# Down projection by halves, two additions left to PSUM, and list masks made as signs on ScalarE

## The chip, the cores and the metric

The kernel runs on one core of a Trainium2 chip. The metric is the device time of one execution in microseconds (us). Throughout, PE is TensorE (its weight loads are shown apart as PEld), DVE is VectorE, ACT is ScalarE, POOL is GpSimd and SP is SyncE, the queue that issues the plain loads and stores. A line number such as L680 is a line of the kernel before.

## The reference

Four sequences of 2048 tokens with 256 features pass through a routed feed-forward layer at half weight, an attention layer and the same feed-forward layer again. The change lies in the two feed-forward layers, which are alike. Each sends every token to two of eight experts; an expert takes the 1280 tokens of its list.

```python
x = x + 0.5 * _L0_ffn_ref(_layernorm(x), router_w, wg, wu, wd)
x = x + _L0_attn_ref(_layernorm(x), Wq, bq, Wk, bk, Wv, bv, Wo, bo)
x = x + 0.5 * _L0_ffn_ref(_layernorm(x), router_w, wg, wu, wd)
# in _L0_ffn_ref, for each expert e and the rows of its list:
g = jnp.einsum('ecd,edf->ecf', disp, wg)                  # 256 -> 1024
u = jnp.einsum('ecd,edf->ecf', disp, wu)                  # 256 -> 1024
eo = jnp.einsum('ecf,efd->ecd', jax.nn.silu(g) * u, wd)   # 1024 -> 256
# each row of eo is multiplied by the token's weight and added to the token's row of the output
```

All of these products are in float32.

## The kernel before

**Chunks and units.** The function `experts` (called once for each feed-forward layer) works through 16 chunks: eight experts, two chunks each, a chunk being 5 tiles of 128 tokens (640 columns, two halves of 320). An expert's chunks are called even (first) and odd (second) below. A chunk has an up stage (`steps_of`) and a down stage (the loop over `order` at the end of `experts`). The up stage has four units `p`. In each unit a 2x2 block product of gate and of up is made from seven half-size products instead of eight: seven pairs of matmuls of 320 columns (`both` is one pair, the gate and the up), with sums of weight blocks (`sums_of_w`, kept in `ws`) and sums of input blocks (`sums_of_x`, kept in `xs`). The results of the pairs are put together by seven additions on DVE, out of PSUM into the tile `ct` (four quadrants of gate and up) by way of `u2`; ACT applies silu to the gate quadrants, and `finish` multiplies gate by up into `h`, on POOL for the first three units and on DVE for the last.

**Down stage.** For each of the 5 token tiles, 8 matmuls of 256 columns are summed in PSUM (h as the stationary side, the expert's `wd` as the moving side). ACT then scales the tile by the tokens' weights into `eo`, and POOL adds it to the tokens' rows in DRAM by an indirect DMA.

**Tokens in.** POOL fetches the rows of a chunk by five indirect DMAs (`gather`, tiles `r`), ACT blanks unused rows (`blank`), PE turns them (`turn`, transposes through the PSUM bank `tr`) and ACT copies them to `xsT`.

**Lists.** `RowList` makes the next expert's list of rows during the even chunk. `high` makes `hi` and `hv` in three DVE instructions; `low(g)`, eight of them, makes a 0/1 mask of 8 x 128 columns from each token's slot number by comparing with a counter on DVE (L395); `products(g)` multiplies the masks in by eight small matmuls; `sum` and `end` bring the sums out, turn them and give the indices `ixs`, for which the gathers of the next expert wait. `behind` places these steps between the token tiles of the down stage. The first list of a layer is made ahead of the chunks by another form of the same functions (`waited_for`).

**Buffers.** In PSUM a pair of banks `mm` is held three times over, `one` and `tr` once each. In SBUF `ct` is held twice: unit `p + 2` writes where unit `p` wrote, and so has to wait until `finish` has read unit `p`. There are 14 buffers `r` and five for the masks `lo`.

**Order.** The chunks run under a manual schedule, in which PE, DVE, ACT and SP keep the order of the source. POOL is left out of it:

```python
with tc.manual_schedule(engines=ENGINES - {mybir.EngineType.Pool}):
```

so the framework's scheduler orders POOL's multiplications and DMAs among themselves. [...]

Of the kernel before, what the change touches and what calls it, by code (L numbers as in the profile page):

```python
# [26 lines left out]
def macaron_kernel(  # L27
# [84 lines left out]

    row_in = const.tile([P, 1], F32, name="row_in")
# [26 lines left out]
    slot_hi = const.tile([P, E, T], I16, name="slot_hi")  # L140

# [130 lines left out]
    def route(w, pool, ppool, beside=iter(())):  # L272
# [73 lines left out]
        nc.vector.tensor_scalar(slot_lo.rearrange("p e t -> p (e t)"), slot, P - 1, None, ALU.bitwise_and)  # L346

    class RowList:
# [4 lines left out]

        def __init__(self, e, pool, ppool, waited_for=False):
            self.e, self.pool, self.ppool, self.waited_for = e, pool, ppool, waited_for
            self.lo = {}
# [26 lines left out]
        def begin(self):  # L383
            self.ps = self.ppool.tile([P, BANK], F32, tag="one", name="ix", bufs=1)[:, :P]

        def low(self, g):
            lo = self.pool.tile([P, TG * P], F16, tag="lo", name="lo", bufs=5)
            at = slot_lo[:, self.e, g * TG : (g + 1) * TG]
            if self.waited_for:
                lo = lo.rearrange("p (s t) -> p s t", t=TG)  # L390
                nc.vector.tensor_tensor(lo, counts, spread(at.unsqueeze(1), [P, P, TG]), ALU.is_equal)
                self.lo[g] = lo.rearrange("p s t -> p t s")
            else:
                shape, lo = [P, TG, P], lo.rearrange("p (t s) -> p t s", s=P)
                nc.vector.tensor_tensor(  # L395
                    lo, spread(count.unsqueeze(1), shape), spread(at.unsqueeze(2), shape), ALU.is_equal
                )
                self.lo[g] = lo
# [10 lines left out]
        def sum(self):  # L409
            self.sums = self.pool.tile([P, P], F32, tag="sums", name="sums", bufs=2)  # L410
            nc.scalar.copy(self.sums, self.ps)

        def end(self):
            self.ps = self.ppool.tile([P, BANK], F32, tag="tr", name="ixT", bufs=1)[:, :P]
            nc.tensor.transpose(self.ps, self.sums, ident)
            ixf = self.pool.tile([P, HI], F32, tag="ixf", name="ixf", bufs=2)
            nc.vector.tensor_reduce(ixf, self.ps.rearrange("p (g i) -> p i g", i=HI), AX.X, ALU.add)
            ix = self.pool.tile([P, HI], I32, tag="ixs", name="ixs", bufs=3)
            nc.vector.tensor_copy(ix, ixf)
            return ix  # L420
# [17 lines left out]
    def experts(name, src, dst, wait_for, weights, wpool, pool, ppool):  # L438
# [4 lines left out]
        PER = ST // CH  # L443
        assert PER == 2 and ST % CH == 0
        chunks = [(e, i) for e in range(E) for i in range(0, ST, CH)]
        lists, got, xTs, turned, ws, xs = {}, {}, {}, {}, {}, {}
        sent = {-1: list(wait_for)}

        def gather(k):
# [4 lines left out]
            for i in range(i0, i0 + CH):  # L454
                r = pool.tile([P, W], F32, tag="r", name="r", bufs=14)
# [32 lines left out]

        def sums_of_w(e, m):
# [10 lines left out]
            tt(o[:, m, 3, :], a12, o[:, m, 1, :], ALU.subtract)  # L500

# [22 lines left out]
        def steps_of(k):  # L524
# [3 lines left out]
            def product(p, m, ps, j, c, b):  # L528
# [5 lines left out]
                nc.tensor.matmul(ps, a, b, start=True, stop=True)  # L534
# [7 lines left out]
            p1 = {}  # L542

            def first_product(p, m):
                if p == NF:
                    return
                one = ppool.tile([P, BANK], F32, tag="one", name="one", bufs=1)
                product(p, m, one[:, :BH], 0, 0, xT[:, 0, :BH])
                if m == 0:
                    p1[p] = pool.tile([P, 2, BH], F32, tag="p1", name="p1", bufs=2)  # L550
                nc.scalar.copy(p1[p][:, m, :], one[:, :BH])  # L551

            first_product(0, 0)
            for p in range(NF):
# [4 lines left out]
                h = pool.tile([P, 2, CH * P], F32, tag="h", name="h", bufs=NF)  # L559
                hq = h.rearrange("p j (t s) -> p (j t) s", t=2)  # L560
# [4 lines left out]
                def finish(engine, qs):  # L565
                    engine.tensor_tensor(hq[:, qs, :], ct[:, qs, 0, :], ct[:, qs, 1, :], ALU.mult)  # L566

                p2 = both(p, 0, 1, xT[:, 1, :BH])
                if p == 0:
                    first_product(0, 1)  # L570
                    if k == 0:
                        rest_of_first()
                    x4 = xs.pop(k)
                tt(ct[:, 0], p1[p], p2, ALU.add)
                if last:
                    silu(slice(0, 1))
                tt(u2, p1.pop(p), both(p, 1, None, x4[:, 1, :]), ALU.add)
                tt(ct[:, 3], u2, both(p, 2, None, x4[:, 2, :]), ALU.add)
                first_product(p + 1, 0)
                tt(ct[:, 2], ct[:, 3], both(p, 1, 1, x4[:, 3, :]), ALU.add)  # L580
                if last:
                    silu(slice(2, 3))
                p5 = both(p, 0, None, x4[:, 0, :])
                tt(ct[:, 1], u2, p5, ALU.add)
                tt(ct[:, 3], ct[:, 3], p5, ALU.add)
                first_product(p + 1, 1)
                if last:
                    silu(slice(3, 4))
                    finish(nc.vector, slice(0, 4, 2))
                tt(ct[:, 1], ct[:, 1], both(p, 3, None, xT[:, 1, BH:]), ALU.add)  # L590
                if last:
                    silu(slice(1, 2))
                    finish(nc.vector, slice(1, 4, 2))
                else:
                    silu(slice(0, 4))
                    finish(nc.gpsimd, slice(0, 4))
                hs.append(h)
                yield hs

        NL = T // TG  # L600

        def beside(k, p):

            if p == 1:
# [3 lines left out]
            if p > 1:  # L608
                turn(k + 1, p - 2)

        def behind(k, i):

            e, step = chunks[k][0], k % PER
            more = following[0] if e + 1 < E else None
            if step == 0 and more:

                if i == 0:
                    more = following[0] = RowList(e + 1, pool, ppool)
                    more.high()
                    for g in range(3):  # L620
                        more.low(g)
                    more.begin()
                elif i == 1:
                    more.products(0)
                    for g in (3, 4, 5):
                        more.low(g)
                elif i == 2:
                    for g in (1, 2, 3):
                        more.products(g)
                    for g in (6, 7):  # L630
                        more.low(g)
                elif i == 3:
                    for g in (4, 5):
                        more.products(g)
                elif i == 3.5:
                    for g in (6, 7):
                        more.products(g)
                    more.sum()
                elif i == 4:
                    lists[e + 1] = more.end()  # L640
                    gather(k + 2)
            elif step == 1:
                if i in (1, 2):
                    sums_of_w(e + 1, i - 1)
                elif i == 3:
                    gather(k + 2)
            if i in (0, 1):
                turn(k + 1, 2 + i)
            elif i == 2:
                sums_of_x(k + 1)  # L650

        following = [RowList(0, pool, ppool, waited_for=True)]
        first = following[0]
        with tc.manual_schedule(engines=ENGINES - {mybir.EngineType.Pool}):
# [14 lines left out]
            for k, (e, i0) in enumerate(chunks):  # L669
                for p, hs in enumerate(steps_of(k)):  # L670
                    beside(k, p)

                order = [(i, p, j) for i in range(CH) for p in range(NF) for j in range(2)]
                order = sorted(order[: 4 * NF], key=lambda o: (o[1] == NF - 1, o[0])) + order[4 * NF :]
                po = {}
                for i, p, j in order:
                    if i not in po:

                        po[i] = banks()[:, 0, :D]
                    nc.tensor.matmul(  # L680
                        po[i], hs[p][:, j, i * P : (i + 1) * P], weights[e][2][:, j * NF + p, :],
                        start=(p == 0 and j == 0), stop=(p == NF - 1 and j == 1),
                    )
                    if i == CH - 1 and (p, j) == (NF // 2, 0):
                        behind(k, i - 0.5)
                    if p < NF - 1 or j == 0:
                        continue
                    eo = pool.tile([P, D], F32, tag="eo", name="eo", bufs=6)
                    nc.scalar.mul(eo, po[i], got[k][i][:, D + e : D + e + 1])  # L689
                    ins = nc.gpsimd.indirect_dma_start(  # L690
                        out=dst[:, :],
                        out_offset=bass.IndirectOffsetOnAxis(ap=lists[e][:, i0 + i : i0 + i + 1], axis=0),
                        in_=eo, in_offset=None, compute_op=ALU.add,
                    )
                    tc.declare_no_dep(ins.ins, group=f"{name}{e}", reason="an expert's rows are distinct")
                    tc.add_to_no_dep_group(f"{name}{e}", ins.ins)
# [475 lines left out]
```

## Time and profile before

| | us |
|---|---|
| median of three runs (2038.27 to 2040.81) | 2039.37 |
| the profiled execution's own time | 2038.74 |
| its span, first to last instruction | 2036.9 |

| engine | busy us | share of the span |
|---|---|---|
| PE | 1875.8 | 92% |
| PEld | 1440.3 | 71% |
| DVE | 1417.6 | 70% |
| ACT | 657.1 | 32% |
| POOL | 883.1 | 43% |

The span holds a first stage (loading and routing, to about 120 us), the first feed-forward layer (to about 920), attention (to about 1140), routing for the second layer (to about 1235) and the second feed-forward layer. Busy times are of the whole span; in the feed-forward layers the shares differ, and the views by stage show them. Matmuls of float32 appear as two records each, and a group's mean duration of one record is longer than the distance from one record to the next, because they overlap on PE.

### The profile page before, as it was taken

The numbers are of one execution on the slowest core, as the hardware profiler recorded it, in microseconds if no ns is written. First come the engines' busy times: TensorE is split into PE (matmuls) and PEld (weight loads), VectorE is DVE, ScalarE is ACT, GpSimd is POOL, SyncE is SP. The second block draws the span as 40 slices with busy tenths as digits, with TensorE's granted clock in tenths as the row PEclk, the third lists the DMA queues.
The fourth block names the chain that finished last, engine by engine and source line by source line (L and its number), as shares of the span: only waits on it lengthen the run. The fifth ranks groups of instructions, "written<-read, shape, count | busy, mean of one in ns | idle before, by whom it ended". The sixth has DMA issues, their size and how long they took to land.

```text
span 2036.9 us, 24719 instructions
## 1 busy us (share of the span) xinstructions
PE 1875.8 (92%) x9176; PEld 1440.3 (71%) x9176; DVE 1417.6 (70%) x2531; ACT 657.1 (32%) x1325; POOL 883.1 (43%) x737
## 2 busy tenths in 40 slices
PE   6379999999999999998999528999999999999998
PEld 4247777777777777777887415777777777777776
DVE  8867676767676767546798886767676676767654
ACT  5322323232223223225565403232222222232221
POOL 5335353535353535335555303535353535353533
PEclk8589999999999999999999858999999999999999
DMA  9902222223131322115002631313232313131211
GB/s 349 302 28 38 78 40 77 57 59 78 38 80 37 79 40 41 17 16 171 32 32 86 206 111 28 79 37 79 39 82 37 82 37 82 35 85 34 43 14 14
DMA packets 99928, 147.63 MB, mean 72 GB/s; under 512 B 7512, under 2 KB 86368, under 8 KB 99680
## 3 DMA queue, kind: packets, MB, share of 16 engines
q1 hardware_dynamic: 69072, 102.77, 15.0%
q0 software_dynamic: 30720, 43.27, 12.9%
q8 instruction: 73, 1.20, 0.3%
q14 instruction: 47, 0.39, 0.1%
q10 hardware_dynamic: 16, 0.01, 0.0%
HBM read 98.84 MB, written 55.57 MB: 76 GB/s over the span
## 4 chain that ended last, share of the span: by engine, by line
PE 83%; DVE 5%; issue 4%; ACT 1%; POOL 1%; DMA 1%; POOLq 0%; DVEq 0%; ACTq 0%; SPq 0%
PE mm L534 41%; PE mm L680 27%; PE one L534 7%; PE tr L481 2%; PE qp L804 1%; PE pc L859 1%; PE ix L404 1%; PE py L917 1%; DVE st L929 1%; DVE xw L927 1%; DVE q L812 1%; DVE m L817 0%; DVE z L826 0%; DVE st L788 0%; PE trq L847 0%
## 5 line engine op out<-in xcount | busy, mean ns | idle before, releaser
L680 PE MATMUL mm<-wdt,h 128*128 128x256 f32 x2560 | 579.0, 381 | 0.0
L680 PEld LDWEIGHTS mm<-wdt,h 128*128 128x128 f32 x2560 | 475.9, 190 | 63.9
L566 POOL TENSOR_TENSOR h<-ct 128x1280 f32<-128x1280 f32 x96 | 279.0, 2906 | 420.2 <-ACT ct L563 417.6
L534 PE MATMUL mm<-xs,ws 128*128 128x320 f32 x1536 | 456.9, 434 | 2.0 <-DVE xs L487 2.0
L534 PEld LDWEIGHTS mm<-xs,ws 128*128 128x128 f32 x1536 | 292.6, 191 | 124.3 <-DVE xs L487 2.5
L487 DVE TENSOR_TENSOR ct<-ct,mm 128x640 f32<-128x640 f32 x384 | 314.4, 819 | 89.4 <-PE mm L534 83.4
L487 DVE TENSOR_TENSOR ct<-p,mm 128x640 f32<-128x640 f32 x128 | 105.1, 821 | 243.4 <-ACT p L551 200.5
L563 ACT ACTIVATE ct<-ct 128x320 f32<-128x320 f32 (+1 forms) x224 | 182.2, 814 | 278.5 <-DVE ct L487 278.5
L487 DVE TENSOR_TENSOR ct<-u,mm 128x640 f32<-128x640 f32 x256 | 210.3, 822 | 61.1 <-PE mm L534 58.0
L551 ACT COPY p<-one 128x320 f32<-128x320 f32 x256 | 109.3, 427 | 405.4 <-PE one L534 404.4
L690 POOL DMA_INDIRECT out_dram<-eo,ixs x80 | 133.1, 1664 | 220.7 <-ACT eo L689 213.7
L690 POOL DMA_INDIRECT acc<-eo,ixs x80 | 132.8, 1660 | 221.2 <-ACT eo L689 214.2
L456 POOL DMA_INDIRECT r<-rows,ixs x160 | 159.0, 994 | 145.0 <-issue 106.5
L689 ACT ACTIVATE eo<-mm,r 128x256 f32<-128x256 f32 x160 | 76.2, 476 | 396.0 <-PE mm L680 396.0
L534 PE MATMUL mm<-xsT,ws 128*128 128x320 f32 x512 | 158.7, 432 | 0.0
L395 DVE TENSOR_TENSOR lo<-count,slot_lo 128x1024 f16<-128x1024 int16 x112 | 128.3, 1220 | 0.0
L534 PEld LDWEIGHTS mm<-xsT,ws 128*128 128x128 f32 x512 | 97.3, 190 | 40.5
L487 DVE TENSOR_TENSOR u<-p,mm 128x640 f32<-128x640 f32 x128 | 104.9, 820 | 17.0 <-PE mm L534 17.0
L534 PE MATMUL mm<-xsT,wgt 128*128 128x320 f32 x256 | 91.0, 437 | 0.0
L534 PE MATMUL one<-xsT,wgt 128*128 128x320 f32 x256 | 91.0, 437 | 0.0
L534 PE MATMUL mm<-xsT,wut 128*128 128x320 f32 x256 | 90.4, 435 | 0.0
L534 PE MATMUL one<-xsT,wut 128*128 128x320 f32 x256 | 89.9, 433 | 0.0
(209 smaller groups left out, 2316.4 us busy)
## 6 DMA issues: line engine op xcount, KB each, us to landing
wgt<-in_L_ffn_wg_dram SPq DMA_DIRECT2D x16, 1024.0 KB, 4.9
wut<-in_L_ffn_wu_dram SPq DMA_DIRECT2D x16, 1024.0 KB, 6.9
wdt<-in_L_ffn_wd_dram SPq DMA_DIRECT2D x16, 1024.0 KB, 5.5
rows<-xw SPq DMA_DIRECT2D x7, 2176.0 KB, 11.8
xw<-in_L_attn_x_dram SPq DMA_DIRECT2D x16, 512.0 KB, 8.8
out_dram<-xw SPq DMA_DIRECT2D x16, 512.0 KB, 2.9
xw<-acc SPq DMA_DIRECT2D x15, 512.0 KB, 8.7
r<-rows,ixs POOLq DMA_INDIRECT x160, 2.8
```

What stands on the lines that cost most here:

```text
L395: nc.vector.tensor_tensor(lo, spread(count.unsqueeze(1), shape), spread(at.unsqueeze(2), shape), ALU.is_equal)
L404: nc.tensor.matmul(self.ps[q, :], self.hv[:, t, :, :], lo[:, t % TG, :], start=(t < Q), stop=(t >= T - Q),)
L456: nc.gpsimd.indirect_dma_start(out=r, out_offset=None, in_=src[:, :], in_offset=bass.IndirectOffsetOnAxis(ap=lists[e][:, i : i + 1], axis=0),)
L481: nc.tensor.transpose(ps[:, (i - i0) * P : (i - i0 + 1) * P], got[k][i][:, c * P : (c + 1) * P], ident)
L487: nc.vector.tensor_tensor(o, a, b, op)
L534: nc.tensor.matmul(ps, a, b, start=True, stop=True)
L551: nc.scalar.copy(p1[p][:, m, :], one[:, :BH])
L563: nc.scalar.activation(ct[:, qs, 0, :], ct[:, qs, 0, :], AF.Silu)
L566: engine.tensor_tensor(hq[:, qs, :], ct[:, qs, 0, :], ct[:, qs, 1, :], ALU.mult)
L680: nc.tensor.matmul(po[i], hs[p][:, j, i * P : (i + 1) * P], weights[e][2][:, j * NF + p, :], start=(p == 0 and j == 0), stop=(p == NF - 1 ...
L689: nc.scalar.mul(eo, po[i], got[k][i][:, D + e : D + e + 1])
L690: ins = nc.gpsimd.indirect_dma_start(out=dst[:, :], out_offset=bass.IndirectOffsetOnAxis(ap=lists[e][:, i0 + i : i0 + i + 1], axis=0), in_ ...
```

## The change

**Down stage by halves.** `wd` is split into 2x2 blocks; `sums_of_wd` makes four sums of them on POOL once an expert (`wds`). `h` is kept as four quadrants of 320 columns, and `sums_of_h` makes four sums of them, on POOL for the first three units and on DVE for the last. The function `down` makes seven products, each of four matmuls of 320 columns, so the result has the features in the partitions. `send` turns it back by ten transposes a chunk through the bank `tr`; ACT scales out of that bank, and POOL adds to DRAM as before. Tiles 0 and 1 are sent ahead of the last two matmuls of their own chunk, tiles 2 to 4 in unit 0 of the next chunk.

**Additions.** In each of the first three units, two of the seven additions are made by letting a product accumulate onto another in PSUM (`onto`); `second_product` lets ACT apply silu straight out of PSUM. The first products of a unit share the pairs of banks `mm`.

**Masks.** `low` makes signs instead of 0/1 masks: 8 ACTIVATE instructions of 129 columns on ACT with a bias from `behind_lo`. `sum` halves the sums and takes differences of neighbours. The list's steps are spread over the units and the down stage (`step_of_list`): `high` and the first mask in the middle of unit 0, one mask in each further unit, four in the down stage.

The diff, cut to its core:

```diff
     class RowList:
...
         def low(self, g):
-            lo = self.pool.tile([P, TG * P], F16, tag="lo", name="lo", bufs=5)
+            lo = self.pool.tile([P, TG * (P + 1)], F16, tag="lo", name="lo", bufs=4)
...
             else:
-                nc.vector.tensor_tensor(
-                    lo, spread(count.unsqueeze(1), shape), spread(at.unsqueeze(2), shape), ALU.is_equal
-                )
+                lo = self.lo[g] = lo.rearrange("p (t s) -> p t s", t=TG)
+                for t in range(TG):
+                    at = behind_lo[:, self.e, g * TG + t : g * TG + t + 1]
+                    nc.scalar.activation(lo[:, t, :], from_below, AF.Sign, bias=at, scale=1.0)
...
         def sum(self):
+                nc.scalar.mul(to, self.ps, 0.5)
+                nc.vector.tensor_tensor(self.sums, to[:, 1:], to[:, :P], ALU.subtract)
...
-                r = pool.tile([P, W], F32, tag="r", name="r", bufs=14)
+                r = pool.tile([P, W], F32, tag="r", name="r", bufs=15)
...
+        def sums_of_wd(e):
+            gt(o[:, 0], a21, a22, ALU.add)
+            gt(o[:, 1], o[:, 0], a11, ALU.subtract)
+            gt(o[:, 2], a11, a21, ALU.subtract)
+            gt(o[:, 3], a12, o[:, 1], ALU.subtract)
+
+        def sums_of_h(op, hq, hT):
+            op(hT[:, 0, :], hq[:, 3, :], hq[:, 1, :], ALU.subtract)
+            op(hq[:, 1, :], hq[:, 1, :], hq[:, 0, :], ALU.subtract)
+            op(hT[:, 1, :], hq[:, 3, :], hq[:, 1, :], ALU.subtract)
+            op(hT[:, 2, :], hq[:, 2, :], hT[:, 1, :], ALU.subtract)
...
+            def first_product(p):
+                ps = both(p, 0, 0, xT[:, 0, :BH])
+                p1 = pool.tile([P, 2, BH], F32, tag="p1", name="p1", bufs=1)
+                nc.scalar.copy(p1, ps)
+                first[p] = ps, p1
+
+            def onto(p, ps, *what):
+                for m in range(2):
+                    product(p, m, ps[:, m, :], *what, start=False)
+                return ps
...
+                def second_product(ps):
+                    c11 = onto(p, ps, 0, 1, xT[:, 1, :BH])
+                    nc.scalar.activation(ct[:, 0, 0, :], c11[:, 0, :], AF.Silu)
+                    nc.scalar.copy(ct[:, 0, 1, :], c11[:, 1, :])
...
+                ps, p1 = first.pop(p)
+                if p > 0 or k == 0:
+                    second_product(ps)
-                tt(ct[:, 0], p1[p], p2, ALU.add)
-                tt(u2, p1.pop(p), both(p, 1, None, x4[:, 1, :]), ALU.add)
+                tt(u2, p1, both(p, 1, None, x4[:, 1, :]), ALU.add)
+                if p == 0 and k > 0:
+                    second_product(ps)
+                early(k, p)
                 tt(ct[:, 3], u2, both(p, 2, None, x4[:, 2, :]), ALU.add)
+                middle(k, p)
                 tt(ct[:, 2], ct[:, 3], both(p, 1, 1, x4[:, 3, :]), ALU.add)
+                late(k, p)
                 p5 = both(p, 0, None, x4[:, 0, :])
-                tt(ct[:, 1], u2, p5, ALU.add)
                 tt(ct[:, 3], ct[:, 3], p5, ALU.add)
...
                 else:
-                    silu(slice(0, 4))
+                    first_product(p + 1)
+                    tt(ct[:, 1], u2, onto(p, p5, 3, None, xT[:, 1, BH:]), ALU.add)
+                    silu(slice(1, 4))
                     finish(nc.gpsimd, slice(0, 4))
+                    sums_of_h(gt, h, hT)
...
+        def early(k, p):
+            if p == 0:
+                send(k - 1, 2, 3)
+            elif p == 1:
+                if k % PER == 0:
+                    sums_of_wd(chunks[k][0])
                 blank(k + 1, 0, 1, 2)
             elif p == 2:
                 blank(k + 1, 3, 4)
+            else:
+                turn(k + 1, 0)
+        def middle(k, p):
+            step_of_list(k, p)
+        def late(k, p):
+            if p == 0:
+                send(k - 1, 4)
+            elif p == 3:
+                turn(k + 1, 1)
+
+        def down(k, hs):
+            own = pool.tile([P, 8, BH], F32, tag="ct", name="y", bufs=2)
...
+            product(c11, block(0, 0), h(0), most)
+            step_of_list(k, 4)
+            product(two[:, 1], summed(2), hT(0), most)
+            step_of_list(k, 5)
+            product(two[:, 0], summed(1), hT(1), most)
+            if second:
+                sums_of_w(e + 1, 0)
+            turn(k + 1, 2)
+            product(c11, block(0, 0), h(0), rest)
+            nc.scalar.copy(p1, c11)
...
+            step_of_list(k, 6)
+            turn(k + 1, 3)
+            product(c11, block(0, 1), h(2), more=True)
+            nc.scalar.copy(own[:, 0, :], c11)
+            step_of_list(k, 7)
+            if second:
+                sums_of_w(e + 1, 1)
+                gather(k + 2)
+            p5 = banks()[:, 0, :BH]
+            product(p5, summed(0), h(1))
...
+            product(p4, block(1, 1), hT(2))
+            tt(own[:, 2, :], u3, p4, ALU.add)
+            step_of_list(k, 8)
+            product(p5, summed(3), h(3), range(NF // 2), more=True)
+            send(k, 0, 1)
+            product(p5, summed(3), h(3), range(NF // 2, NF), more=True)
+            tt(own[:, 1, :], u2, p5, ALU.add)
+            step_of_list(k, 9)
```

In the changed program as built, POOL's instructions of an even and the following odd chunk, where a next expert exists, stand so: two additions to DRAM (tiles 0 and 1 of the chunk before), the four sums of `wd`, three additions (tiles 2 to 4), the multiplications and sums of the even chunk's three units, two additions (tiles 0 and 1 of the even chunk), seven gathers, two additions, two gathers, one addition, one gather, and then the multiplications and sums of the odd chunk's three units.

## The prediction

> **What bounds the kernel now.** I read the page's costliest groups first, then the busy time of each engine in stretches of 100 us, then the chain that ended last. The groups name PE's two products, with means of single records that overlap:
>
> ```profile
> L680 PE MATMUL mm<-wdt,h 128*128 128x256 f32 x2560 | 579.0, 381 | 0.0
> ...
> L566 POOL TENSOR_TENSOR h<-ct 128x1280 f32<-128x1280 f32 x96 | 279.0, 2906 | 420.2 <-ACT ct L563 417.6
> L534 PE MATMUL mm<-xs,ws 128*128 128x320 f32 x1536 | 456.9, 434 | 2.0 <-DVE xs L487 2.0
> ```
>
> A stretch within the feed-forward layer (busy PE, PEld, DVE, ACT, POOL, then PE's clock) shows PE without a gap at full clock, the others far from full:
>
> ```profile
> 600.00:700.00 100.00, 100.00 (x473) 75.96 (x472) 69.37 (x91) 30.47 (x62) 44.73 (x27) 1.00 0.26 59
> ```
>
> The chain (start, duration, what) gives the real distance between records and the period of a pair of chunks:
>
> ```profile
> 598.00 6.46 PE mm L534 x24
> 604.68 6.05 PE mm L680 x28
> ...
> 697.24 6.46 PE mm L534 x24
> ```
>
> 6.46/24 = 0.269 us for 320 columns, 6.05/28 = 0.216 for 256; a pair of chunks takes 697.24 - 598.00 = 99.24. So PE's instructions are the time here, and anything that makes PE wait is added whole.
>
> [...] at 786.10 below, POOL multiplies only once the DMAs ahead of it are through. [...] after the idle time before the first chunk; two pairs at 1.07 each, later 0.54:
>
> ```profile
> 121.66 1.27 PE L534 MATMUL one<-xsT,wgt 128*128 128x320 f32 x2
> 122.73 1.27 PE L534 MATMUL mm<-xsT,wgt 128*128 128x320 f32 x2
> 123.80 0.74 PE L534 MATMUL mm<-xsT,wut 128*128 128x320 f32 x2
> 124.37 0.70 PE L534 MATMUL one<-xsT,wut 128*128 128x320 f32 x2
> ```
>
> [...] 2906/1280 = 2.27 ns in the trace[...].
>
> **Part 1, PE's own work.** The up stage keeps its 56 matmuls a chunk. Down: 80 records x 0.216 = 17.28 become 56 x 0.269 = 15.07, plus 10 transposes back at 0.11 (597.73 to 597.84 in the timeline) = 1.1. Gain 1.1 a chunk, 32 chunks: **-36**. The 64 small list matmuls (129 for 128 columns) I take as equal.
>
> **Part 2, POOL ahead of the odd chunk.** The present timeline of POOL at an odd chunk's start, after a list:
>
> ```profile
> 773.13 1.56 POOL L690 DMA_INDIRECT acc<-eo,ixs  x1 [2.87 <-ACT eo L689]
> 774.99 1.01 POOL L456 DMA_INDIRECT r<-rows,ixs  x1 [0.30 <-issue]
> ...
> 785.12 0.95 POOL L456 DMA_INDIRECT r<-rows,ixs  x1 [0.31 <-issue]
> 786.10 2.91 POOL L566 TENSOR_TENSOR h<-ct 128x1280 f32<-128x1280 f32 x1
> ```
>
> The odd chunk began at 772.3; unit 0's multiplication came 13.8 later, one addition and nine gathers ahead of it, and just in time. In the changed program five additions (1.58 + 0.30 gap) and ten gathers (0.95 + 0.30) stand there: 9.4 + 12.5 = 21.9, from 0.2 before the chunk's start, when tile 0's scaled rows are ready. Unit 0's multiplication runs 21.5 to 24.4. Who waits: unit 2 writes into unit 0's `ct`, first by ACT's silu and copy from PSUM, which also free the bank pair of the unit's first product. PE's slots of 4 records are 1.08. With six transposes (0.65) in unit 0, it and unit 1 end at 16.8; unit 2's accumulation and two products end at 20.0; its next product needs that bank, free at 24.4 + 0.1 + silu 0.47 + copy 0.43 = 25.4. **PE waits 5.4.** Later it is covered: unit 1's `ct` is free at 30.2, wanted at 31.1; unit 2's sums end near 39 (twelve new sums a chunk at 320 x 2.27 = 0.73), wanted from 38. That is 7 odd chunks a layer, 14 in all: **+76**. [...] half clock may follow: [...] I take 1.0, about what the cold rows lost: **+14**.
>
> **Part 3, `high` in unit 0 of the even chunk.** It now stands on DVE between the second and third product's additions:
>
> ```profile
> 755.47 1.22 DVE L376 TENSOR_TENSOR hi<-count,slot_hi 128x1024 f16<-128x1024 int16 x1
> 756.73 0.49 DVE L380 TENSOR_SCALAR hv<-hi,row_in 128x1024 f16<-128x1024 f16 x1
> 757.13 1.22 DVE L381 TENSOR_TENSOR hv<-hi,row_of 128x1024 f16<-128x1024 f16 x1
> 758.26 1.22 DVE L395 TENSOR_TENSOR lo<-count,slot_lo 128x1024 f16<-128x1024 int16 x1
> ```
>
> 758.26 - 755.47 = 2.79. DVE starts 0.20 after a product's slot ends (slot to 786.83, DVE at 787.03):
>
> ```profile
> 785.75 1.24 PE L534 MATMUL mm<-xs,ws 128*128 128x320 f32 x4
> ...
> 786.83 0.70 PE L534 MATMUL one<-xsT,wut 128*128 128x320 f32 x2
> 787.03 0.82 DVE L487 TENSOR_TENSOR ct<-u,mm 128x640 f32<-128x640 f32 x1 [0.26 <-PE mm L534]
> ...
> 790.67 1.30 ACT L470 ACTIVATE r<-r 128x256 f32<-128x256 f32 x3
> ```
>
> From the chunk's start: second product's addition 4.9 to 5.7, `high` to 8.5, then two additions of 0.82 (0.74 apart) to 10.05. PE wants to accumulate onto the bank that the last of them reads at 8.2: it waits **1.9**, x 14 = **+27**. The wait is new; `high` stood in the down stage, where DVE was not awaited. Whether POOL's sums of `wd`, then running, slow DVE the trace doesn't show: 0 to 2.
>
> **Part 4, signs on ACT.** No ACTIVATE of 129 columns is in the trace. The nearest are L470's three above: (1.30 - 0.50)/2 = 0.40 apart at 256 columns; less 127 x 0.83 ns (the slope of L563's 320 and 1280 columns) = 0.30. [...] I take 0.30, so eight take 2.45[...]. In the units they hide in ACT's idle time: unit 1's first product is ready 7.0 after the unit's start, the blanks and signs are through at 6.7. In the down stage ACT first ends the last unit's silu, 2.7 after the stage's start (in the present timeline the up stage's last slot ends at 703.53, that silu at 706.18), so the fifth mask is ready at 5.15, and PE asks for it after six matmuls of 0.54 and one list step of 0.2, at 3.45: **1.7** wait, x 14 = **+24**[...]. The later masks then keep pace. The masks' 8 x 1.22 leave DVE, as do 7 additions of 0.82 a chunk; both are off the path, so worth nothing, and five additions of 320 columns and four sums come to DVE in the down stage, hidden too except 0.35 in odd chunks, where eight sums for the next weights go ahead: 16 x 0.35 = **+6**. The even chunk's POOL work fits: multiplications end at 16, 24 and 32 against 19, 27 and 35 wanted.
>
> **Part 5, ends.** The last chunk's rows:
>
> ```profile
> 2027.16 0.47 ACT L689 ACTIVATE eo<-mm,r 128x256 f32<-128x256 f32 x1 [2.98 <-PE mm L680]
> 2027.91 1.56 POOL L690 DMA_INDIRECT out_dram<-eo,ixs  x1 [1.89 <-ACT eo L689]
> ```
>
> Today only one addition follows PE's last product, through 2.5 after it. Then five queue at 1.88: through at 8.9. **+6.4 a layer, +13**, since the first layer's attention loads wait for them too. A layer's first chunk has no product between first and second: 0.9 each, **+2**.
>
> **Sum.** -36 + 76 + 14 + 27 + 24 + 6 + 13 + 2 = +126. The profiled execution took 2038.74 (span 2036.9), 0.63 below the median: 2038.7 + 126 = 2164.7; against the median **2165**.
>
> **Rivals.** *All covered, faster*: POOL comes to unit 0 in time, and `high` and signs are hidden: -36 + 13 + 2 gives **2018**. It decides at 16: if the fifteen DMAs average below 1.1 us instead of 1.45, nobody waits. Against it, the same gaps stand in every group of gathers. Chance 0.06. *Only POOL's queue counts* (masks quicker, `high` absorbed): 2039 - 36 + 15 + 90 = **2108**; for it, my list-chunk waits rest on tenths; 0.18. *Dearer waits*: [...] **2219**; 0.18. That the change is not what it says: the built order has seven four-matmul products and five additions in three units of four, and no more table loads (four in each program); excluded.
>
> **How the numbers follow.** The main case has 0.58, with its own range 2130 to 2195. The range **2095 to 2222** takes in the last two rivals. Faster by over 0.2% (about what a measurement of this kernel can tell from no change) 0.06, within it 0.02, slower 0.92.
>
> **What would show it.** Right: PE gaps of about 5 us in seven odd chunks a layer, with ACT waiting for POOL's `h` in unit 2; a pair of chunks near 107 us; about 2 us gaps in unit 0 of even chunks behind DVE, and before the fifth mask; last pairs, without a list, near 97. Wrong: PE full in the odd chunks, or gaps in every unit of every chunk, which would mean accumulating onto a bank is too tight (0.05 spare by my slots).

## The result, and the profile after

The changed kernel takes 2270.34 us in the median of four runs (2269.19 to 2273.91) against 2039.37: a ratio of 1.1135, 95% interval 1.1116 to 1.1154. The profiled execution has a span of 2267.5 us against 2036.9, so 230.6 more, where the prediction had 126. From here on, line numbers are those of the kernel that is spoken of; in the changed kernel L570 is the up stage's matmul and L744 the down stage's.

Among the costliest groups of the page (busy us, mean ns of one, then idle time ahead of it and what ended it), PE's matmul groups, which had next to no idle time before, now have some:

```profile
L407 ACT ACTIVATE lo<-from_below,behind_lo 128x129 f16<-128x129 f32 x896 | 272.7, 394 | 0.0
L570 PE MATMUL mm<-xsT,ws 128*128 128x320 f32 x512 | 183.1, 483 | 53.6 <-DVE ct L502 53.6
...
L570 PE MATMUL mm<-xs,wgt 128*128 128x320 f32 x256 | 104.4, 492 | 70.0 <-ACT ct L609 70.0
```

The two waits, 53.6 and 70.0, are both on the path, and by the waits view each is made of 14: fourteen of 5.0, and twelve of 4.1 with two of 2.2 in the layers' first chunks. In the stretch that was full before, PE is now idle for 5%, at a mean clock of 0.95, and does 402 matmuls where it did 473. DVE is less busy too (51.92 for 69.37): the work taken from it stood beside PE.

```profile
600.00:700.00 100.00, 94.55 (x402) 62.96 (x402) 51.92 (x78) 45.29 (x116) 56.95 (x46) 0.95 0.19 45
```

The chain gives the length of the runs of matmuls: at full clock 24 records take 6.76; the first 24 of unit 2 in an odd chunk take 8.85, and 16 in unit 0 of an even chunk take 7.21, where both_behind, below, has 4.57.

```profile
598.49 7.21 PE mm L570 x16
...
614.00 6.76 PE mm L570 x24
...
671.42 8.85 PE mm L570 x24
```

A pair of chunks takes mostly 113.8 and 114.9 in turn (mean 114.4), measured from one list's last transposition to the next; before it was 99.24.

**The odd chunk's wait.** PE's timeline (start, duration, what, idle time ahead and what ended it) shows the wait and, behind it, 4.3 us at half clock (two records in 1.1 instead of 0.54) until 675.70:

```profile
671.42 1.43 PE L570 MATMUL mm<-xs,wgt 128*128 128x320 f32 x2 [4.99 <-ACT ct L609]
672.65 1.27 PE L570 MATMUL mm<-xs,wut 128*128 128x320 f32 x2
673.72 2.15 PE L570 MATMUL mm<-xs,ws 128*128 128x320 f32 x4
675.70 0.70 PE L570 MATMUL mm<-xsT,wgt 128*128 128x320 f32 x2
```

POOL's timeline has the cause as predicted. The chunk began at 645.9; five additions and ten gathers stand ahead of unit 0's multiplication, which starts 21.8 later (predicted 21.5):

```profile
645.78 1.58 POOL L687 DMA_INDIRECT acc<-eo,ixs  x1 [18.50 <-ACT eo L686]
...
666.69 0.97 POOL L471 DMA_INDIRECT r<-rows,ixs  x1 [0.30 <-issue]
667.70 2.88 POOL L604 TENSOR_TENSOR h<-ct 128x1280 f32<-128x1280 f32 x1
```

**The even chunk's wait.** In unit 0 PE waits 4.1 for DVE, predicted 1.9. DVE's timeline shows why: `hi` takes 2.50 instead of 1.22, the first `hv` 1.38 instead of 0.49.

```profile
591.74 2.50 DVE L386 TENSOR_TENSOR hi<-count,slot_hi 128x1024 f16<-128x1024 int16 x1
594.27 1.38 DVE L390 TENSOR_SCALAR hv<-hi,row_in 128x1024 f16<-128x1024 f16 x1
595.57 1.21 DVE L391 TENSOR_TENSOR hv<-hi,row_of 128x1024 f16<-128x1024 f16 x1
```

In POOL's timeline the third and fourth sum of `wd` run at that very time; the second `hv`, for which they are over, takes its usual 1.21:

```profile
591.31 1.84 POOL L505 TENSOR_TENSOR wds<-wds,wdt 128x512 f32<-128x512 f32 x1
593.23 2.14 POOL L505 TENSOR_TENSOR wds<-wdt,wds 128x512 f32<-128x512 f32 x1
```

The prediction held that the trace before doesn't show whether POOL slows DVE. In unit 0 it doesn't; but in the attention stage it does. A DVE instruction of the same line, tiles and shape takes 0.79 beside a POOL instruction of 128 x 512 with two operands in SBUF, and 0.29 at 1151.95, where POOL is idle:

```profile
1062.62 1.06 POOL L829 TENSOR_TENSOR q<-q,rz 128x512 f32<-128x512 f32 x1
1063.03 0.79 DVE L220 TENSOR_TENSOR p<-tmp,mx 128x128 f32<-128x128 f32 x1
...
1151.95 0.29 DVE L220 TENSOR_TENSOR p<-tmp,mx 128x128 f32<-128x128 f32 x1
```

**The fifth mask and the end** are as forecast. The fifth mask's eight small matmuls take 2.17 on PE where the others' take 0.30, and eight signs take 2.45 on ACT:

```profile
621.50 2.45 ACT L407 ACTIVATE lo<-from_below,behind_lo 128x129 f16<-128x129 f32 x8
...
629.64 2.17 PE L413 MATMUL ix<-lo,hv 128*32 128x129 f16 x8
```

After PE's last product (its slot ends at 2251.17) the fifth addition to DRAM is issued until 2260.08, so 8.9 later.

### The profile page after: what moved, and what is told of

It is laid out like the page before. It is cut to its first block, busy times and chain, and to the rows that moved or that the text cites. A ratio compares the mean times of both kernels' runs of the same rounds, so it can differ in the third digit from the quotient of the medians.

```text
span 2267.5 us, 25439 instructions
## 1 busy us (share of the span) xinstructions
PE 1955.2 (86%) x8728; PEld 1349.9 (60%) x8728; DVE 1309.2 (58%) x2497; ACT 970.1 (43%) x2381; POOL 1299.9 (57%) x1188
## 4 chain that ended last, share of the span: by engine, by line
PE 65%; DVE 15%; POOL 7%; ACT 4%; issue 4%; DMA 1%; POOLq 0%; DVEq 0%; SPq 0%; ACTq 0%
PE mm L570 37%; PE mm L744 18%; DVE ct L502 4%; POOL r L471 2%; POOL h L604 2%; PE tr L496 2%; POOL out_dram L687 1%; ACT lo L407 1%; PE back L681 1%; POOL acc L687 1%; DVE hi L386 1%; PE ix L413 1%; PE qp L911 1%; PE pc L966 1%; PE py L1024 1%
## 5 line engine op out<-in xcount | busy, mean ns | idle before, releaser
L570 PE MATMUL mm<-xs,ws 128*128 128x320 f32 x1536 | 479.0, 443 | 2.0 <-DVE xs L502 2.0
L570 PEld LDWEIGHTS mm<-xs,ws 128*128 128x128 f32 x1536 | 292.9, 197 | 114.0 <-issue 15.2
L601 ACT ACTIVATE ct<-ct 128x960 f32<-128x960 f32 (+1 forms) x192 | 141.4, 736 | 342.3 <-DVE ct L502 342.3
L407 ACT ACTIVATE lo<-from_below,behind_lo 128x129 f16<-128x129 f32 x896 | 272.7, 394 | 0.0
L570 PE MATMUL mm<-xsT,ws 128*128 128x320 f32 x512 | 183.1, 483 | 53.6 <-DVE ct L502 53.6
L584 ACT COPY p<-mm 128x640 f32<-128x640 f32 x128 | 88.6, 692 | 262.8 <-PE mm L570 262.8
L570 PE MATMUL mm<-xsT,wgt 128*128 128x320 f32 x512 | 187.9, 450 | 1.6 <-ACT p L584 1.6
L570 PE MATMUL mm<-xsT,wut 128*128 128x320 f32 x512 | 185.3, 444 | 0.0
L505 POOL TENSOR_TENSOR hT<-h 128x320 f32<-128x320 f32 x192 | 172.4, 898 | 15.1
L570 PEld LDWEIGHTS mm<-xsT,ws 128*128 128x128 f32 x512 | 95.3, 202 | 117.2 <-DVE ct L502 83.6
L570 PE MATMUL mm<-xs,wgt 128*128 128x320 f32 x256 | 104.4, 492 | 70.0 <-ACT ct L609 70.0
L744 PE MATMUL mm<-h,wds 128*128 128x320 f32 x512 | 156.5, 438 | 0.0
L744 PE MATMUL mm<-hT,wds 128*128 128x320 f32 x512 | 154.4, 440 | 1.1 <-DVE hT L502 0.5
L744 PE MATMUL mm<-h,wdt 128*128 128x320 f32 x512 | 153.6, 433 | 0.0
```

The lines of the kernel that those rows point to most:

```text
L407: nc.scalar.activation(lo[:, t, :], from_below, AF.Sign, bias=at, scale=1.0)
L505: nc.gpsimd.tensor_tensor(o, a, b, op)
L570: nc.tensor.matmul(ps, a, b, start=start, stop=True, skip_group_check=not start)
L584: nc.scalar.copy(p1, ps)
L601: nc.scalar.activation(ct[:, qs, 0, :], ct[:, qs, 0, :], AF.Silu)
L744: nc.tensor.matmul(ps, a(p), b(p), start=(p == 0 and not more), stop=(p == NF - 1), skip_group_check=more)
```

## The experiments

The theory at this point: the miss is one of size, not of place. The waits stand where they were forecast, but DVE and POOL slow each other in unit 0 of the even chunk (`hi` 2.50 for 1.22), and half clock follows every wait of 4.1 and 5.0. Rivals: PE's new products are slower in themselves (accumulating onto a bank, the list's 129 columns), or the tail carries it. gathers_behind, high_late and warm_odd change one thing each in the changed kernel, before_signs one in the kernel before; the others build on each other as said.

**1. gathers_behind: the queue ahead of the odd chunk.**

```diff
-        def gather(k):
+        def gather(k, behind=()):
...
+                after(ins, behind, "behind the units' products")
...
             if second:
                 sums_of_w(e + 1, 1)
-                gather(k + 2)
+                gather(k + 2, held[-1:])
```

`held` collects POOL's last sum of `h` in each unit, so `held[-1:]` is the latest, that of unit 2.

> The changed kernel, but the five gathers that belong to the odd chunk's own down stage are tied behind the sums of its unit 2 on POOL, so ten DMAs instead of fifteen stand ahead of unit 0's multiplication (5 x 1.88 + 5 x 1.25 = 15.7 us, ending near 15.5 after the chunk's start). Queue theory: the 5.0 us wait in unit 2 of the 14 odd chunks goes, and with it the half clock after it (24 records in 8.3 to 8.9 us instead of 6.46, 2.1 on average): 2270 - 14 x 7.1 = 2171. Rival, the wait only moves (unit 3's buffer or the later gathers become the late ones): less than half of that, 2220 or more.

Measured: 2176.01, ratio 1.0666 (1.0648 to 1.0684). A pair takes 107.5, so 6.9 less than 114.4: the wait of 5.0 and 1.8 of half clock. PE no longer waits in the odd chunk; the even chunk's wait stays at 53.6 in 14. The queue is shown.

**2. both_behind: also the sums of `wd` out of the way of `high`.**

```diff
-            gt(o[:, 0], a21, a22, ALU.add)
+            ins = gt(o[:, 0], a21, a22, ALU.add)
+            after(ins, held[-1:], "behind unit 0's sums")
...
-            gt(o[:, 2], a11, a21, ALU.subtract)
+            ins = gt(o[:, 2], a11, a21, ALU.subtract)
+            after(ins, held[-1:], "behind unit 0's sums")
```

> As gathers_behind, and the four sums of wd are tied behind unit 0's sums on POOL, so that POOL only issues DMAs while DVE makes hi and hv in unit 0 of the even chunk. Theory that POOL's two-input sums slow DVE's (hi 2.50 against 1.22, hv 1.38 against 0.49): the three DVE instructions take 2.8 again, the wait in unit 0 falls from 4.2 to 1.9 and the half clock after it (2.3 us on average) goes: 2171 - 14 x 4.6 = 2107. Rival, the slow hi is due to ACT's masks or the order of the operands and not to POOL: it stays at 2.5, and the time stays within 10 us of gathers_behind.

Measured: 2118.41, ratio 1.0381 (1.0363 to 1.0399), 58 less than gathers_behind. The instructions on DVE are the same and in the same order, but they have their old durations again, in DVE's timeline:

```profile
656.09 1.22 DVE L386 TENSOR_TENSOR hi<-count,slot_hi 128x1024 f16<-128x1024 int16 x1
657.34 0.49 DVE L390 TENSOR_SCALAR hv<-hi,row_in 128x1024 f16<-128x1024 f16 x1
```

PE's wait is now the forecast 1.9 (27.4 in 14), and mostly no half clock follows it; in three of the twelve pairs it does, and they take 104.7 instead of 102.85. Then 16 records take 6.27 instead of 4.57, so 1.7 more. In the pair shown it sets in 1.18 after PE has resumed: the first four records are at full clock, the next two take 1.22 instead of 0.70:

```profile
453.11 1.34 PE L577 MATMUL mm<-xsT,ws 128*128 128x320 f32 x4 [1.91 <-DVE ct L503]
454.29 1.22 PE L577 MATMUL mm<-xsT,wgt 128*128 128x320 f32 x2
```

So it was POOL's sums that made DVE slow. It goes both ways: from the third sum's start to the fourth's 1.92 passed in the changed kernel, 1.35 here (673.22 to 674.57). From the start of `hi` to that of the second `hv` it was 3.83, here 1.65 (656.09 to 657.74). An estimate from these numbers: at the start of `hi` POOL still had about 2.2 of its own sums to do (1.35 and 1.27, begun 0.43 earlier), and 1.65 + 2.2 is the 3.83. So side by side the two engines were through no sooner than one behind the other.

`hi`, with two SBUF inputs, was slowed by a factor of 2 (1.22 to 2.50), the first `hv`, with one SBUF tensor input, by 2.8 (0.49 to 1.38); the additions of 0.82, with one input in PSUM, kept their duration beside POOL's sums and multiplications in the changed kernel (0.81 to 0.82). Which property of the inputs decides, these traces do not show.

**3. high_late: the other way to the same wait.** `high` goes behind unit 0's addition that PE waits for; the sums of `wd` stay.

```diff
             if n == 0:
                 following[0] = RowList(e + 1, pool, ppool)
-                following[0].high()
                 following[0].begin()
...
                 tt(ct[:, 3], ct[:, 3], p5, ALU.add)
+                if p == 0 and k % PER == 0 and e + 1 < E:
+                    following[0].high()
```

> The changed kernel, but hi and hv are made after unit 0's fourth addition (that on which PE's accumulation waits) instead of ahead of it; POOL's order as in the changed kernel. Theory that their place makes PE wait: the wait of 4.2 falls to about 0.5 (the fifth addition is late and holds up a bank in unit 1), and the half clock after it goes: 2270 - 14 x 6.0 = 2186. Rival, the wait is due to something else in unit 0 (the transposes back, ACT's copies): within 20 us of 2270.

Measured: 2200.73, ratio 1.0792 (1.0774 to 1.081). The wait in unit 0 is gone (in all 6.6 are left of 53.6), `hi` with a mean of 1.46 is still slowed in part, and the odd chunk's wait (65.6) stays. It gains 70 where 84 was expected; part of the rest, 6, is dearer half clock in the odd chunk, whose 24 records take 9.05 in the mean instead of 8.62. What else it is was not found.

**4. warm_odd: half clock alone.** Ten records of dummy matmuls fill the odd chunk's wait.

```diff
         def early(k, p):
...
             elif p == 2:
                 blank(k + 1, 3, 4)
+                if k % PER and chunks[k][0] + 1 < E:
+                    stay_busy(ppool.tile([P, BANK], F32, tag="one", name="warm", bufs=1), 5)
```

> The changed kernel with five matmuls of 512 columns on constants (0.86 us each, 4.3 in all, results not used) put into unit 2 of the 14 odd chunks that have a list before them, where PE waits 5.0 anyway. Theory that the slow records after the wait come from PE's idleness: they run at full clock (24 records in 6.5 us), 2270 - 14 x 2.1 = 2241, and the granted clock rises from 0.926. Rival, the clock falls for another reason or the added matmuls lengthen the wait: 2270 or more.

Measured: 2261.38, ratio 1.1082 (1.1063 to 1.11), so 9 less instead of 29; a pair takes 113.2, 1.1 less. PE's timeline has the dummies, and behind them the 24 records take 6.83 by the chain, 2.0 less than 8.85. But two waits stand in the same chunk's down stage that the changed kernel does not have:

```profile
663.99 4.45 PE L160 MATMUL warm<-row_of_ones,ident 128*128 128x512 f32 x10
...
685.84 0.81 PE L746 MATMUL mm<-hT,wds 128*128 128x320 f32 x2 [0.21 <-POOL hT L505]
```

The second is for DVE, 0.27 at 687.78. The down stage of that chunk takes 17.20 for 16.06. POOL, 5 us behind its time, was the next limit; a faster PE reaches it. So the idle time does bring the half clock, and it costs these 24 records 2.0, but about half of that was hidden behind POOL's delay. (14 x 1.1 is 16, not 9: the first chunks of the two layers took 6 longer here. They differ by 2 to 4 from kernel to kernel, which was not followed up.)

**5. lag, on top of both_behind: the fifth mask.**

```diff
-            if 0 < n <= NL:
-                more.products(n - 1)
+            if 2 <= n <= NL + 1:
+                more.products(n - 2)
...
-            elif n == NL:
+            elif n == NL + 1:
                 more.sum()
```

> This kernel is both_behind (2118) with one change: the list's products of mask g come two steps after the signs of mask g instead of one, the sum in the middle of the last product and the list's transposition at its end. Theory (the fifth mask is signed behind the last unit's silu, and PE, asking for it too early, waits 1.4 us in each of 14 even chunks): the row of eight products of 1.70 becomes about 0.4, 14 x 1.3 = -18, 2100; a pair of chunks 101.5 instead of 102.9. Rival (what the list costs is PE's own 64 small products and their changes of weights): no change, 2118. A third: the last mask, now asked for at the end of the stage, is late instead, and the wait moves there: 2110 to 2118.

Measured: 2106.16, ratio 1.0327 (1.0307 to 1.0347); most pairs take 101.9. The row of eight products is at 0.30 again, in PE's timeline:

```profile
370.77 0.30 PE L413 MATMUL ix<-lo,hv 128*32 128x129 f16 x8
```

12 less of 18, in runs that lie 10 apart: the wait was for signs that stand late in ACT's queue. Of the third expectation a little is there, PE's transposes behind the next group wait 0.25 for an ACT copy (375.33).

**6. no_onto, on both_behind: the accumulation onto a bank.**

```diff
+                    tt(ct[:, 1], u2, p5, ALU.add)
                     first_product(p + 1)
-                    tt(ct[:, 1], u2, onto(p, p5, 3, None, xT[:, 1, BH:]), ALU.add)
+                    tt(ct[:, 1], ct[:, 1], both(p, 3, None, xT[:, 1, BH:]), ALU.add)
```

> This kernel is both_behind (2118) with one change: in the first three units the seventh product gets its own pair of banks and DVE adds it (two additions of 0.82 more on DVE), instead of PE accumulating onto the fifth product's pair. Theory (an accumulation onto a pair that DVE has still to read ties PE to DVE: 0.10 in each of 96 units, and the whole 1.9 us wait behind high in 14 even chunks): -10 - 27 = 2081, with the rows of four records at 1.24 instead of 1.34 and no wait over 0.5 in unit 0 of even chunks. Rival A (the 1.9 us is DVE's lateness, whichever bank it reads: with three pairs the next product needs one that DVE frees later still): only the 0.10s go, 2108. Rival B (DVE with one addition more a unit gets later): 2118 or slower.

Measured: 2099.32, ratio 1.0282 (1.0264 to 1.03), 19 less of the 37. The rows of four records are at 1.24 again instead of 1.34, and the wait in unit 0 falls from 1.9 to 1.0 (14.4 in 14). But DVE, with its addition more, is late in the down stage, by PE's timeline:

```profile
632.39 1.34 PE L752 MATMUL mm<-hT,wds 128*128 128x320 f32 x4 [0.32 <-DVE hT L503]
```

The theory and both rivals hold in part: the accumulation ties PE to DVE, half of the wait in unit 0 is DVE's lateness whichever bank it reads, and the time that the accumulation took from DVE is wanted elsewhere.

**7. lag_split, on lag: `high` in three pieces,** one behind the seventh product's addition of unit 0, two in unit 1.

```diff
                 tt(ct[:, 3], ct[:, 3], p5, ALU.add)
+                if p == 1:
+                    piece_of_high(k, 1)
...
                     tt(ct[:, 1], u2, onto(p, p5, 3, None, xT[:, 1, BH:]), ALU.add)
+                    if p < 2:
+                        piece_of_high(k, 2 * p)
```

> This kernel is lag with one change more: high, 2.9 us of DVE in one piece between two additions of unit 0 of the even chunk, is cut into its three operations, put behind the seventh product's addition of unit 0, the fifth's of unit 1 and the seventh's of unit 1, where a product without a DVE reader follows. Theory (the 1.9 us wait of unit 0 comes from the piece's length and place, not from its work): that wait goes, 14 x 1.9 = -27 against lag, 2073, a pair of chunks 99.6. Rival (DVE has no room for it in any unit): the wait is split too, 0.5 to 0.8 in three places, 2085 to 2100.

Measured: 2075.74, ratio 1.0166 (1.0149 to 1.0183); a pair takes 100.0. 30 less: the wait came from the piece's length and place.

**8. all_three: lag_split with no_onto's edit.**

> This kernel is lag_split with the seventh product of the first three units added by DVE, as in no_onto. If no step of the changed kernel is dearer than these waits, what is left over the kernel before is its ends (about 20 us) and the list's products (about 1 us a list), against a gain of 36 in the down products: 2073 - 10 = 2063. Theory: 2063, a pair of chunks 99.0. Rival (with the room in DVE gone again, the pieces of high make the additions late): 2075 or more.

Measured: 2073.5, ratio 1.0152 (1.0135 to 1.0169), not to be told from lag_split. The records are at 1.24 again, but in the odd chunk's down stage PE waits for DVE, 0.34 of it ahead of the transposes at 630.35: what the tie costs comes back as DVE's lateness.

With the waits gone, PE's own time can be read. In lag_split the odd chunk without a list takes 48.03 (48.52 before), the even one with a list 51.97 (50.71 before). So the list costs 3.9 where it cost 2.2; 0.2 of the 3.9 is a wait for POOL's `h` in the down stage (2.8 in 14).

**9. grouped, on lag_split: the list's products two masks at a time.**

```diff
-            if 2 <= n <= NL + 1:
-                more.products(n - 2)
+            if n in (3, 5, 7, 9):
+                more.products(n - 3)
+                more.products(n - 2)
```

> This kernel is lag_split (2075.7) with one change: the list's products are issued two masks at a time (after the third up unit's third product, and three more times), in four groups of 16, instead of eight groups of 8 between other products. In lag_split a list chunk takes PE 51.97 against 48.03 without a list, so 3.9 a list; in the kernel before, with four groups, 2.2. Theory (PE pays for every change between the 320-column products and the list's, about 0.2 to 0.25 on each side, not for the small products): four changes fewer save 1.2 to 1.7 a list, x 14 = -17 to -24: 2055, a pair of chunks 98.7. Rival (the 64 products of 129 columns on signs cost PE more in themselves than those of 128 on zeros and ones): no change, 2076.

Measured: 2069.11, ratio 1.0132 (1.0115 to 1.0149), 7 less instead of 17 to 24. A new wait has taken the rest, in PE's timeline:

```profile
660.44 0.81 PE L769 MATMUL mm<-h,wdt 128*128 128x320 f32 x2 [0.53 <-POOL h L618]
```

**10. wd_late, on grouped: POOL's last sum of `wd` behind unit 2's sums.**

```diff
-            gt(o[:, 3], a12, o[:, 1], ALU.subtract)
+        def last_of_wd(e):
...
+            ins = gt(o[:, 3], a12, o[:, 1], ALU.subtract)
+            after(ins, held[-1:], "behind unit 2's sums")
...
+                if k % PER == 0:
+                    last_of_wd(chunks[k][0])
                 turn(k + 1, 0)
```

> This kernel is grouped (2069.1) with one change: the last of the four sums of wd, 1.27 on POOL and needed only by the last down product, goes behind the third unit's sums instead of ahead of the second unit's. In grouped PE waits 0.53 for POOL's h and 0.25 for what DVE makes of it later, at the down stage of every list chunk. Theory (grouping the list's products did save PE its changes, and POOL, unchanged, then became late): both waits go, 14 x 0.8 = -11, 2058, a pair of chunks 98.9. Rival (the waits come from POOL's transfers, not from these sums): 2069. Against the kernel before it is slower in both cases, by about 18 or 29 us, which is the longer ends of both layers (about 25) and the dearer list (about 5), less the gain of the down products.

Measured: 2059.38, ratio 1.0089 (1.0075 to 1.0103). A pair takes 99.35, and POOL's wait is gone. One is left for DVE, whose last unit now runs beside POOL's sums (`h` there 1.36 and 1.08, sums up to 1.44, that take 0.82 and 0.49 alone):

```profile
668.11 1.34 PE L775 MATMUL mm<-hT,wds 128*128 128x320 f32 x4 [1.01 <-DVE hT L510]
```

A pair now costs what it cost before (99.24). The 23 us by which the span is longer are the ends: 9.8 from the last list of the first layer to the first of the second, 6.3 in the tail, 5.3 around the first chunks, and 1.4 in the pairs.

**11. before_signs: the third part alone, on the kernel before.**

```diff
         def beside(k, p):
+            if k % PER == 0 and chunks[k][0] + 1 < E:
+                if p == 0:
+                    following[0] = RowList(chunks[k][0] + 1, pool, ppool)
+                following[0].low(p)
```

Masks and sums are made as in the changed kernel.

> This kernel is the kernel before with the third part of the change alone: masks as signs on ACT (129 columns, 8 operations a mask, half the difference of neighbours at the end), four of a list's eight masks signed after the four up units and four in the down stage, where DVE made all eight in the down stage; its list products stay in groups of 8, 24, 16 and 16. Theory (what the changed kernel lost by its signs is only the wait for the fifth mask; the eight masks of 1.22 us that DVE no longer makes were beside PE, so worth nothing): no wait here where the products lag, 2040, within 10. Rival (2.45 us of signs in ACT's queue hold up ACT's copies out of the single bank of the first products and the scaling of the rows): a wait of 1 to 3 us in each of 14 even chunks, 2055 to 2085.

Measured: 2083.94 against 2043.98 for the kernel before in the same series, so 40 more, ratio 1.02 (1.0175 to 1.0225). The rival won. In the waits view (total, times, longest), PE's transposes of the next tokens wait for a copy that stands behind signs in ACT's queue:

```profile
PE tr L492 <- ACT xsT L495: 27.4, 17, 1.8
```

In ACT's queue, at these places, the signs are no free work, even where DVE's masks were. Of these waits 14 are of 1.84, one in each list chunk, and behind five of them PE runs at half clock, which costs 1.7 each, 8 in all. What is left was not taken apart.

## Why the prediction was right or wrong

The direction held, and the places of the waits did; the size did not: 2270 lies outside the range of 2095 to 2222, whose upper end rested on the author's own estimates of dearer signs and half clock. The terms of the sum, with what the runs show beside them:

| step | predicted | measured |
|---|---|---|
| odd chunk's wait for POOL (Part 2) | 76 | 70.0 (14 of 5.0) |
| half clock behind it (Part 2) | 14 | 25 (24 records at 8.62 in the mean, 6.83 in warm_odd) |
| even chunk's wait for DVE (Part 3) | 27 | 53.6 (12 of 4.1, two of 2.2) |
| half clock behind that | 0 | 29 (16 records at 6.61 in the mean, 4.57 in both_behind) |
| fifth mask (Part 4) | 24 | 26 (2.17 - 0.30, x 14) |
| list's small matmuls | 0 | 24 (lag_split: 3.9 - 2.2, x 14; 3 of it is that wait for POOL, which the changed kernel doesn't have) |
| accumulating onto the bank | 0 | 10 (1.34 - 1.24, in 96 units) |
| first lists of the layers | 0 | 9 (PE waits 16.6 for `lo` of L401, 7.8 before; 8.6 in both_behind; POOL's sums of the first `wd` run there from 104.85 on, beside DVE's first masks) |
| ends (Part 5) | 15 | 14 (attention's first transposes 14.0 for 7.8 behind the last product, then half clock of 1.8; tail 8.9 for 2.5) |
| PE's own work, and the odd chunk's additions | -30 | -30 (not measured apart: lag_split's odd chunk fits it, -1.1 + 0.35 + 0.3 = -0.45 against -0.49) |

The column sums to 231, or 228 without POOL's 3, against 230.6 of span; its terms come from several traces, and the last is taken from the prediction, so a few us of this agreement are luck.

**Step 1 that failed: the term left open in Part 3.** "Whether POOL's sums of `wd`, then running, slow DVE the trace doesn't show: 0 to 2" was the right question with the wrong value taken: it is 2.2 (4.1 against 1.9 in twelve of fourteen), and the 0 went into the sum. What to take could have been read from the trace before, where a DVE instruction goes from 0.29 to 0.79 beside POOL. The prediction's own arithmetic of that wait is right where POOL is out of the way, 1.9 in both_behind.

**Step 2: half clock.** It was put in for the odd chunk alone, at 1.0. That a wait of 1.9 stays free of it was the author's estimate; the trace before does not show it. The wait became 4.1, and then the even chunk pays as well, 2.0 in the mean beside the odd chunk's 1.8. In the changed kernel waits of 4.1 and 5.0 bring half clock every time, and so did the two of 2.2; it also followed three of both_behind's twelve of 1.9 and five of before_signs' fourteen of 1.84. So the length alone doesn't decide; what else does stays open. Steps 1 and 2 together are 53.6 + 29 - 27 + 11 = 67 of the 105 missing, and both_behind less gathers_behind shows 58 for the even chunk's part.

**Step 3: "The 64 small list matmuls I take as equal."** Their number is; but eight groups stand where four did, and 21 to 24 us is what that and the rest of the list cost. grouped and wd_late recover part of it, 7 and about 9, the second by ending POOL's lateness. **Step 4: "0.05 spare"** for the accumulation was not there: such a row takes 1.34 where it takes 1.24 in no_onto.

Right were the length of POOL's queue and who waits behind it (21.8 for 21.5, 5.0 for 5.4), the duration of a sign (0.30 apart, eight in 2.45), the fifth mask's wait and the ends. That DVE's freed time buys nothing fits too (its busy time fell by 108 and the kernel became slower), as far as the masks go: before_signs takes them off DVE and gains nothing.

## What to carry to other kernels

A product saved on PE is worth its slots only if every engine that feeds it keeps its old margin: here 36 us of matmuls were to be saved, and the extra work on POOL, ACT and DVE cost several times that through waits of 2 to 5 us, with half clock behind all 28 of 2.2 to 5.0. Where an estimate of a wait comes near these lengths, cost the clock behind it too, here 1.4 to 3.1 each time. And before a step is moved beside another engine's work, look in the trace for the same instruction at times when that engine is busy and when it is idle, as the 0.79 and 0.29 above: one that gets longer there was no free place.

## What the runs showed of the hardware

- DVE and POOL slowed each other while POOL ran sums of two SBUF operands (changed kernel against both_behind): `hi` of 128 x 1024, with two SBUF inputs, from 1.22 to 2.50, the one-input `hv` in 16 bits from 0.49 to 1.38, POOL's sum of 128 x 512 from 1.35 between two starts to 1.92. Together they took about as long as one behind the other (3.83 against 1.65 + 2.2, the 2.2 an estimate from both_behind's 1.35 and 1.27). DVE's additions with an operand in PSUM stayed at 0.82.
- Half clock came behind every wait of 4.1 or 5.0 on PE and behind both of 2.2 (changed kernel, 28 waits in its chunks), and behind 3 of 12 of 1.9 (both_behind) and 5 of 14 of 1.84 (before_signs). In the changed kernel it cost 1.4 to 3.1 each time (odd chunk: 8.26 to 9.04 for 6.83; even chunk: 6.04 to 7.64 for 4.57).
- A change from 320-column float32 matmuls to the list's small 16-bit ones and back cost PE about as much as a group of eight of these itself: the group takes 0.42 of PE, 0.23 itself and 0.1 more on each side (lag_split's timeline, 652.44 to 652.86 beyond the slots of the products around it). Whether the type or the shape brings it was not tried.
